# Four graph layers for 32 batches: how the last pair's attention weights are turned, weighed and divided

## The chip, the cores and the metric

The kernel runs on one core of one Trainium2 chip. Its engines work side by side, each through its own list of instructions in order: TensorE (PE, with its weight loads PEld), VectorE (DVE), ScalarE (ACT), GpSimd (POOL) and SyncE (SP), which here issues nearly all DMAs. The metric is the device time of one execution in microseconds (us); times on a profile page count from the start of the span.

## The reference

x has 32 batches of 512 nodes with 64 features; adj is a 512 x 512 graph with about 2% of its entries set. Four layers each add to x a function of h = relu(layernorm(x)). Layers 0 and 1 multiply by the graph and by small matrices. Layers 2 and 3 are attention:

```python
# layer 2: eight heads of the first gat_layer, then one more on their concatenation
h = x @ W
s = einsum('bnd,bmd->bnm', h, h) * graph
s = where(s == 0.0, -1e16, s)
a = softmax(s, axis=2)
out = einsum('bnm,bmd->bnd', a, h) + b          # leaky_relu 0.01 behind it
# layer 3
h = x @ weight
e = leaky_relu(h @ a[:D] + (h @ a[D:]).T, 0.2) * adj   # adj with ones on its diagonal
out = einsum('bij,bjd->bid', softmax(e), h) + bias
```

So each attention needs for every node a maximum over 512 scores, 512 exponentials and their sum, and then a sum of 512 rows of values weighed by the exponentials. TensorE can form that sum only with the weights turned, so that the summed node lies on the partitions.

## The kernel before, in words

Batches go in 16 pairs. A pair passes through `front` (layers 0 and 1 and the layer norms, in steps F0 to F32), the heads of layer 2 (units a, b, c, d, g, h, i, j; two units make a `Two`), the second attention of layer 2 (called f, or O), and layer 3 (called e, or L). Pairs overlap: while one is in its heads, the one before is in its O and L.

Every piece of work is a *job* with a name such as `15.x0O1` (pair 15, exponentials 0 of the O attention of batch 1). The order in which the jobs are written out is a list in the code: HEAD for the start, ROUND, which is repeated with a lag per job, and TAIL for the end, which begins in the middle of pair 12's heads. Nothing else orders the work: an engine takes its instructions as the list of jobs issues them, and waits at each for its inputs and for a free buffer. The letters: s scores, r maxima, m negated maxima, x exponentials, n normalise, t turn, v weigh, then u evict, t rows, r residual; oA, oB and oC are the layer norm behind O, oT, oE, oN and oV turn its result and form layer 3's values, de its target terms; aO and aL fetch rows of the graph; hQ, lQ and ZQ spread values over partitions by DMA. PSUM has four banks for scores and four for everything else; `mm_ps` gives a job the bank whose present user comes earliest in the list, by the table UNTIL.

An attention unit in general: scores come to PSUM; DVE (L678) multiplies them by the graph's factor and takes the maximum in one pass, at 128 rows x 512; POOL negates (L691); ACT takes exponentials with their sum (L698); DVE takes the reciprocal (L708) and POOL multiplies the 512 weights by it (L710); DVE turns blocks of 32 x 32 (L716); TensorE weighs with 32-row tiles (L725 for the heads, L953 for O and L of two neighbouring pairs). The 32-row tiles need the values with node 32 b + r on partition r, which the DMAs of `Spread` (L474) arrange.

The last pair has no neighbour behind it. Its O and L are cut into halves, one per batch (`Half`, L1026, with `HalfOut`, L1075, and `HalfLast`, L1133), of four tiles of 128 nodes, so that a batch can go on to layer 3 alone. A half of the last pair goes: scores (L1082 and L1087 for O; for L, targets at L1137 and then one ACT instruction per tile, L1143), maxima, negation for two tiles at a time, exponentials, normalisation on POOL, 32x32 turns on DVE, and then `weigh` (L1050): 64 matmuls with 32 x 64 values as weights and 128 columns of turned weights moving, into four PSUM banks. ACT (for L half of it DVE) evicts with the bias, L1067 and L1065; four TensorE turns (L1072) make rows of nodes again; DVE adds the residual (L1095, or L1150 with the output's DMA at L1151). The values for `weigh` are spread by `SpreadRows`: a store to DRAM (L1018) and four reads (L1023) per half, on SP's queue.

The other lines that are spoken of: L552 and L871 form layer 3's features and terms of pair 14, L863, L878 and L903 are SP's DMAs of its source and target terms (src, dst, pd), L907 its scores on ACT. L482 turns pair 14's result back, L934 and L935 add and store it. L1107 and L1117 are turns and layer 3's features of a half of pair 15; L504 is the aggregation over the graph in `front`; L820 turns a half's values.

Of the kernel before, what the change touches and what calls it, by code (L numbers as in the profile page):

```python
# [21 lines left out]
def gnn_stack_kernel(  # L22
# [36 lines left out]
        w03:y03 w13:y13 o3:c3 vAE:eu et:er oT:oE oN:oV oD:oF h0:H0 h1:H1 vAL:lu lt:lr vAO0:ouO0 otO0:orO0 oT0:oE0  # L59
        oN0:oV0 vAL0:ouL0 otL0:orL0 vAO1:ouO1 otO1:orO1 oT1:oE1 oN1:oV1 vAL1:ouL1 otL1:orL1  # L60
    """
    HEAD = """
        0.weights 0.F0 0.F1 0.F2 0.biases 0.F3 0.F4 0.joined 0.F5 0.F6 1.F0 0.graph3 0.graph0 0.graph1 1.F1 0.graph2
        0.F7 0.F8 0.bjoined 0.F9 0.F10 0.F11 0.F12 0.F13 0.F14 1.F2 0.F15 0.factor0 0.masks 0.F16 0.F17 0.grams
        0.F18 0.F19 0.F20 0.F21 0.F22 0.F23 2.F0 0.F24 0.F25 1.F3 0.factor1 0.factor3 0.F26 0.F27 1.F4 0.F28 1.F5
        1.F6 0.F29 1.F7 0.loops0 0.F30 0.F31 0.loops2 0.F32 0.zT 1.F8 0.zE 1.F9 0.vectors 0.k0 1.F10 0.Y0 0.factor2
        0.ZQ03 0.ZQ12 0.k1 0.s1a 0.s0a 0.r3a 0.r2a 0.r1a 0.r0a 0.ZQ02 0.m1a 0.s3a 0.r6a 0.r7a 0.x1a 0.s2a 0.m0a
        0.r4a 0.s1b 0.r5a 0.r2b 0.m3a 0.r3b 0.m2a 0.s0b 0.x0a 0.s2b 0.nAa 0.ZQ11 0.Y1 0.ZQ01 0.x2a 0.r0b 0.x3a 0.r1b
        0.r5b 0.m1b 0.k3 0.s1c 0.r4b 0.m0b 0.x1b 0.t0a 0.s3b 0.t1a 0.nBa 0.r3c 1.F11 0.r7b 0.x0b 0.r6b 0.m3b 0.t2a
        0.m2b 0.x3b 0.nAb 0.r2c 0.s3c 0.t3a 0.x2b 0.r6c 0.m1c 0.s2c 0.ZQ13 0.r7c 0.nBb 1.F12 0.Y3 0.x1c 1.F13 0.t0b  # L70
        0.t1b 1.F14 0.k2 0.ZQ00 0.Y2 0.t3b 0.s0c 0.t2b 0.r5c 0.r0c 0.vA0 0.r4c 0.r1c 0.s3d 0.m3c 0.m0c 0.m2c 0.s0d
        0.x3c 0.vB0 0.r0d 0.vC0 0.r1d 0.x0c 0.vD0 0.nAc 0.s1d 0.t0c 0.x2c 0.r6d 0.m0d 0.r7d 0.nBc 0.t1c 0.r3d 0.s2d
        0.us0 0.w10 0.r2d 0.r5d 0.r4d 0.w00 0.m3d 0.s1g 0.m1d 0.x0d 0.x1d 0.t3c 0.m2d 0.r2g 0.y10 0.nAd 0.s3g 0.x3d
        0.r3g 1.F15 0.x2d 0.r7g 0.t2c 0.r6g 0.nBd 0.y00 0.t1d 1.F16 0.m1g 0.t0d 0.o0 1.F17 0.t2d 0.s0g 0.m3g 0.c0
        0.x3g 0.t3d 1.F18 0.loops1 0.s0h 0.x1g 0.r1h 0.r0h 1.F19 0.vA1 0.vB1 1.F20 0.r0g 0.vC1 0.m0h 0.vD1 0.s2g
        0.r1g 0.s1h 0.us1 0.r5g 0.r4g 0.m0g 0.x0g 0.w01 1.F21 0.m2g 0.nAg 0.x2g 0.y01 0.w11 0.r2h 0.r3h 0.ZQ10 0.s3h
        0.m1h 2.F1 0.s2h 1.F22 0.x0h 0.x1h 0.nBg 0.t0g 0.y11 0.r7h 0.r6h 0.s0i 0.r5h 1.F23 1.F24 0.m3h 0.r4h 0.x3h
        0.m2h 0.nAh 0.t2g 1.F25 0.s1i 0.x2h 0.t1g 0.t3g 0.r1i 0.r2i 0.o1 0.t0h 0.nBh 0.t1h 1.F26 0.s2i 0.c1 0.r0i
        0.r3i 1.F27 0.t2h 0.t3h 1.F28 1.F29 0.s3i 2.F2 0.m1i 0.vA2 0.m0i 0.r5i 0.r4i 1.F30 0.m2i 0.x0i 0.r6i 0.vB2
        0.D0 0.x2i 1.F31 0.vC2 0.vD2 0.s1j 0.r7i 0.x1i 0.r3j 0.r2j 0.us2 1.F32 0.m3i 0.s0j 1.zT 3.F0 2.F3 1.zE  # L80
        1.ZQ01 0.m1j 0.s2j 0.r1j 0.r5j 0.w12 0.r0j 0.nAi 0.m0j 0.x3i 2.F4 0.r4j 0.nBi 0.s3j 2.F5 0.r7j 0.m2j 0.r6j
        0.t0i 0.y12 2.F6 1.k0 0.t1i 1.Y0 0.w02 0.m3j 1.s1a 1.s0a 1.r2a 1.r3a 0.x0j 0.x1j 2.F7 0.t2i 0.nAj 0.x2j
        1.r0a 0.t3i 0.t0j 1.m1a 0.x3j 0.y02 1.s2a 1.ZQ02 0.nBj 2.F8 1.r1a 1.k1 1.Y1 0.t1j 0.o2 1.s3a 0.t2j 0.t3j
        0.c2 1.ZQ00 1.r6a 0.vA3 1.r7a 1.r5a 1.s1b 1.m0a 1.r4a 1.m2a 1.s0b 1.m3a 0.vB3 1.x0a 1.r2b 1.x1a 0.vC3 1.nAa
        3.F1 1.x3a 1.x2a 1.nBa 1.r3b 1.r1b 1.r0b 1.t1a 1.m1b 0.vD3 1.s3b 1.m0b 1.ZQ03 1.t0a 1.r7b 0.f0 0.us3 1.s2b
        1.x1b 1.r6b 1.r4b 2.F9 1.x0b 0.loops3 1.r5b 1.s0c 0.w03 1.r0c 1.r1c 1.m2b 1.m0c 2.F10 1.s2c 1.nAb 1.r4c
        1.x2b 0.y03 1.r5c 1.m3b 1.t2a 1.s1c 0.w13 0.y13 1.r3c 1.x3b 1.t0b 1.r2c 2.F11 0.o3 1.nBb 2.F12 1.m2c 2.F13
        1.s0d 1.s3c 1.t1b 1.m1c 1.t3a 1.t2b 0.c3 0.f1 2.F14 1.t3b 1.r1d 1.r7c 0.hQ0 1.x0c 1.vA0 1.x2c 1.ZQ12 1.r0d
        1.r6c 1.s2d 1.m3c 1.m0d 1.x1c 1.nAc 0.D1 1.s1d 1.r3d 1.r2d 3.F2 1.r4d 1.m1d 1.x0d 1.t0c 1.r5d 1.vB0 1.x1d
        1.vC0 1.nAd 1.vD0 1.us0 1.m2d 1.t1c 1.s3d 1.x3c 1.r7d 1.r6d 0.s1f 1.nBc 1.t0d 1.m3d 0.r3f 1.w10 0.r2f 1.k2  # L90
        1.y10 1.Y2 0.hQ3 0.s0f 1.w00 2.F15 1.x2d 1.x3d 1.t1d 1.t2c 1.nBd 0.r1f 1.t3c 1.y00 0.s2f 1.t2d 0.m1f 2.F16
        1.t3d 2.F17 0.hQ2 0.r4f 2.F18 1.o0 0.s3f 0.x1f 1.c0 2.F19 0.r0f 0.r6f 4.F0 0.r5f 0.r7f 1.vA1 0.m0f 1.vB1
        0.x0f 0.m2f 2.F20 1.s0g 1.ZQ13 0.hQ1 1.s2g 1.vC1 1.vD1 0.m3f 1.r0g 1.r4g 2.F21 1.s3g 0.x2f 0.nAf 1.r5g 1.m2g
        1.us1 1.r1g 1.s1g 1.w01 0.x3f 1.w11 1.y01 1.r6g 1.m0g 1.r7g 1.s0h 0.t1f 1.r2g 0.nBf 0.t0f 1.y11 1.r3g 1.x0g
        0.t2f 1.x2g 1.m1g 1.r0h 2.F22 0.t3f 1.m3g 1.x1g 1.o1 1.s1h 1.r1h 1.nAg 2.F23 1.t0g 1.x3g 2.F24 1.nBg 1.ZQ10
        1.m0h 2.F25 1.s3h 1.c1 1.r7h 1.r3h 1.x0h 0.vAE 0.vBE 0.vCE 0.vDE 1.r2h 1.s2h 0.eu 1.t1g 1.t3g 1.r6h 1.m1h
        1.t2g 1.k3 1.r4h 1.m3h 0.et 1.Y3 1.r5h 1.x1h 1.s1i 1.m2h 0.er 1.s0i 1.x2h 1.ZQ11 1.x3h 1.r2i 1.nAh 1.r1i
        1.r0i 2.F26 1.s3i 1.t0h 1.nBh 2.F27 1.r3i 1.t1h 1.s2i 1.t2h 1.r6i 2.F28 1.r4i 1.m1i 1.m0i 1.x0i 1.x1i 1.s1j
        2.F29 1.t3h 2.F30 1.r5i 1.r7i 1.vA2 1.m3i 1.r3j 1.D0 1.m2i 1.x2i 1.vB2 2.F31 1.x3i 2.F32 1.vC2 1.nBi 1.r2j
        1.vD2 1.s2j 1.m1j 1.nAi 0.oA 1.r5j 1.us2 2.zT 2.zE 1.s0j 1.r4j 1.m2j 1.s3j 3.F3 1.w12 1.x1j 1.hQ0 3.F4 1.r1j  # L100
        1.hQ1 1.r0j 1.t3i 1.y12 1.m0j 4.F1 1.r6j 1.r7j 2.k0 1.w02 1.m3j 2.Y0 1.x0j 2.s0a 3.F5 1.t2i 3.F6 1.y02 0.oB
        2.s1a 2.r1a 2.k1 2.r0a 1.x2j 1.t0i 1.nAj 2.m0a 2.s2a 2.r3a 1.x3j 2.Y1 2.r2a 2.r5a 2.r4a 2.m2a 1.nBj 3.F7
        1.t1i 3.F8 1.t0j 1.t2j 1.o2 2.s3a 1.t1j 2.s1b 1.c2 1.f0 2.m1a 1.t3j 1.vA3 2.x1a 2.x0a 1.vB3 2.x2a 2.r2b
        2.nAa 2.r6a 1.vC3 1.vD3 2.r7a 2.m3a 2.x3a 2.s0b 2.t0a 2.r3b 2.t1a 1.us3 2.nBa 3.F9 2.r1b 2.ZQ03 3.F10 2.r0b
        2.ZQ02 1.w03 2.m0b 2.s3b 1.y03
    """
    ROUND = """
# [782 lines left out]
    class Last(Unit):  # L890
# [34 lines left out]
        def rows(self):  # L925
            self.pn = turned(self.yT)
# [449 lines left out]
```

## Time and profile before

| | us |
|---|---|
| median of 3 runs | 2054.76 (2052.51 to 2057.88) |
| the profiled execution | 2054.5 |
| its span, first to last instruction | 2052.6 |
| busy PE, DVE, ACT, POOL in the span | 1998.0, 1813.9, 1491.9, 1304.4 |
| mean granted TensorE clock | 0.992 |

The page has a line per engine with the span in 40 slices of 51 us, a digit for the tenths in which it was busy:

```profile
PE   6999999999999999999999999999999999999986
DVE  4788889999898999989899998999999899899965
ACT  1567678777787877778777787877778687777855
POOL 3466566757667576666757567675866766566543
PEclk9999999999999999999999999999999999999997
```

A row of the timeline or of the groups is to be read as: line, engine, operation, output<-inputs, tile (rows * columns of TensorE where there is one), partitions x elements, count. TensorE takes a float32 matmul in two records; a turn of 128 x 128 in one. A busy PE is not PE at its peak, since its matmuls overlap.

### The profile page before, as it was taken

The numbers are of one execution on the slowest core, as the hardware profiler recorded it, in microseconds if no ns is written. First come the engines' busy times: TensorE is split into PE (matmuls) and PEld (weight loads), VectorE is DVE, ScalarE is ACT, GpSimd is POOL, SyncE is SP. The second block draws the span as 40 slices with busy tenths as digits, with TensorE's granted clock in tenths as the row PEclk, the third lists the DMA queues.
The fourth block names the chain that finished last, engine by engine and source line by source line (L and its number), as shares of the span: only waits on it lengthen the run. The fifth ranks groups of instructions, "written<-read, shape, count | busy, mean of one in ns | idle before, by whom it ended". The sixth has DMA issues, their size and how long they took to land.

```text
span 2052.6 us, 91028 instructions
## 1 busy us (share of the span) xinstructions
PE 1998.0 (97%) x38941; PEld 1201.2 (59%) x38941; DVE 1813.9 (88%) x4170; ACT 1491.9 (73%) x3845; POOL 1304.4 (64%) x2211
## 2 busy tenths in 40 slices
PE   6999999999999999999999999999999999999986
PEld 4556565665656566565656656566565565665555
DVE  4788889999898999989899998999999899899965
ACT  1567678777787877778777787877778687777855
POOL 3466566757667576666757567675866766566543
PEclk9999999999999999999999999999999999999997
DMA  6101111111121110212111021211111121111222
GB/s 139 33 3 35 22 31 39 36 25 37 26 41 31 36 37 19 45 25 43 29 34 38 17 45 27 43 33 31 35 23 36 27 49 33 34 30 31 41 47 65
DMA packets 257625, 74.45 MB, mean 36 GB/s; under 512 B 240324, under 2 KB 249668, under 8 KB 257220
## 3 DMA queue, kind: packets, MB, share of 16 engines
q1 hardware_dynamic: 256768, 68.54, 16.1%
q8 instruction: 305, 5.00, 1.0%
q14 instruction: 100, 0.82, 0.1%
q10 hardware_dynamic: 452, 0.10, 0.0%
HBM read 16.52 MB, written 4.78 MB: 10 GB/s over the span
## 4 chain that ended last, share of the span: by engine, by line
PE 90%; DVE 4%; ACT 2%; issue 1%; DMA 1%; POOL 1%; SPq 0%; POOLq 0%; ACTq 0%; DVEq 0%
PE s L669 23%; PE mm L725 23%; PE mm L504 6%; PE s L672 6%; PE mm L527 5%; PE mm L786 5%; PE mm L953 5%; PE mm L766 5%; PE mm L1169 3%; PE mm L530 3%; DVE sm L678 2%; PE mm L552 2%; DVE sm L716 2%; PE mm L492 1%; PE mm L521 1%
## 5 line engine op out<-in xcount | busy, mean ns | idle before, releaser
L698 ACT ACTIVATE sm<-sm,nmx 128x512 f32<-128x512 f32 x1280 | 909.6, 716 | 183.0 <-POOL nmx L691 181.4
L710 POOL TENSOR_SCALAR sm<-sm,rs 128x512 f32<-128x512 f32 x1280 | 866.2, 696 | 231.0 <-DVE rs L708 212.4
L678 DVE CUSTOM_DVE_ANT_0 sm<-s,A 128x512 f32<-128x512 f32 x1264 | 803.7, 679 | 49.7 <-PE s L672 44.0
L716 DVE STREAM_TRANSPOSE sm<-sm 128x1024 f32<-128x1024 f32 x640 | 775.4, 1229 | 52.6 <-POOL sm L710 49.8
L669 PE MATMUL s<-ZZ,Y 64*64 64x512 f32 x4096 | 553.9, 597 | 1.6 <-DVE mx L678 0.9
L725 PE MATMUL mm<-sm,vq 32*64 32x256 f32 (+1 forms) x16640 | 485.8, 376 | 2.6 <-DVE rs L708 1.8
L725 PEld LDWEIGHTS mm<-sm,vq 32*64 32x64 f32 x16640 | 384.7, 132 | 117.7 <-issue 52.5
L691 POOL TENSOR_SCALAR nmx<-mx 128x2 f32<-128x2 f32 x640 | 131.1, 216 | 361.2 <-DVE mx L678 328.9
L698 ACT ACTIVATION_READ_ACCUMULATOR sm<-sm,nmx 128x1 f32 x1280 | 246.9, 193 | 0.0
L672 PE MATMUL s<-NEGM,I2b 64*64 64x512 bf16 x2288 | 242.2, 376 | 0.0
L669 PEld LDWEIGHTS s<-ZZ,Y 64*64 64x64 f32 x4096 | 144.2, 133 | 163.4 <-issue 72.2
L778 ACT ACTIVATE y<-mm,cols 128x512 f32<-128x512 f32 x256 | 161.2, 688 | 26.3 <-PE mm L766 26.1
L672 PEld LDWEIGHTS <-I2b 64*64 64x64 bf16 x2288 | 80.2, 107 | 152.2 <-issue 150.9
L447 POOL TENSOR_TENSOR r<-ve,mhalf 128x8 f32<-128x8 f32 (+1 forms) x65 | 106.3, 1636 | 49.8 <-DVE ve L445 49.7
L766 PE MATMUL mm<-us,Wh 64*64 64x512 f32 x1024 | 133.8, 590 | 1.5 <-ACT us L760 1.4
L760 ACT COPY us<-mm 128x256 f32<-128x256 f32 x256 | 75.9, 380 | 70.0 <-PE mm L725 69.9
L786 PE MATMUL mm<-y,Wo_sb 128*64 128x256 f32 x1024 | 124.1, 384 | 2.5 <-ACT Y L1180 2.5
L504 PE MATMUL mm<-AT,z 128*128 128x512 f32 x256 | 119.9, 612 | 4.5 <-DVE z L451 4.2
L527 PE MATMUL mm<-AT,v 128*64 128x256 f32 x1024 | 117.6, 382 | 0.1
L953 PE MATMUL mm<-sm,vq 32*64 32x256 f32 x3712 | 111.8, 376 | 2.0 <-DVE rs L708 0.7
L953 PEld LDWEIGHTS mm<-sm,vq 32*64 32x64 f32 x3712 | 101.5, 132 | 15.9 <-PE s L672 7.9
L678 DVE DVE_READ_ACCUMULATOR2_ANT mx<- 128x1 f32 x1280 | 106.0, 83 | 0.0
(166 smaller groups left out, 1849.0 us busy)
## 6 DMA issues: line engine op xcount, KB each, us to landing
vq<-z SPq DMA_DIRECT2D x512, 32.0 KB
HH<-cat SPq DMA_DIRECT2D x128, 64.0 KB
vq<-catT SPq DMA_DIRECT2D x240, 32.0 KB
vq<-h3n SPq DMA_DIRECT2D x240, 32.0 KB
A<-in_adj_dram SPq DMA_DIRECT2D x5, 1024.0 KB
xt<-in_x_dram SPq DMA_DIRECT2D x32, 128.0 KB
ZZ<-ZZ SPq DMA_DIRECT2D x32, 128.0 KB
out_dram<-xo SPq DMA_DIRECT2D x32, 128.0 KB
```

The costliest lines, as they stand in the source:

```text
L504: nc.tensor.matmul(pe, lhsT=v[:, m].rearrange("p j d -> p (j d)"), rhs=AT[:, m, :], start=(m == 0), stop=(m == NT - 1),)
L527: nc.tensor.matmul(ph[out_, :], lhsT=v[:, m, j, :], rhs=AT[:, m, h], start=False, stop=stop)
L669: nc.tensor.matmul(pss[half][R[ab], :], lhsT=lhsT, rhs=rhs, start=True, stop=False)
L672: nc.tensor.matmul(pss[half][R[ab], :], lhsT=I2b[R[half], :], rhs=NEGM[R[half], k, :], start=False, stop=True)
L678: nc.vector.tensor_tensor_reduce(self.sm[:, s, :], self.pss.pop(s), self.graph(s), 1.0, -FMAX, ALU.mult, ALU.max, self.small("mx", slice(s ...
L698: nc.scalar.activation(self.sm[:, s, :], self.sm[:, s, :], AF.Exp, bias=self.small("nmx", slice(s, s + 1)), accum_out=self.small("ssum", s ...
L710: nc.gpsimd.tensor_scalar(self.sm[:, s, :], self.sm[:, s, :], self.small("rs", slice(s, s + 1)), 1.0, ALU.mult, ALU.mult)
L716: nc.vector.transpose(out=two, in_=two)
L725: nc.tensor.matmul(self.u[i][R[c], 0 : weights.shape[1] * 32], lhsT=values[32 * i : 32 * i + 32, jb, :], rhs=weights[32 * i : 32 * i + 32, ...
L766: nc.tensor.matmul(self.py[ab][c][r, :], lhsT=Wh2[R[c], self.head(c, ab), r], rhs=self.us[R[c], 2 * ab : 2 * ab + 2].rearrange("p i (s e) ...
L786: nc.tensor.matmul(self.pa[R[half], 0 : N // 2], lhsT=Wo_sb[:, self.head(k, ab), :], rhs=self.y[self.head(k, ab)][:, half * N // 2 : (half ...
L953: nc.tensor.matmul(self.u[i][r, 0 : N // 2], lhsT=values[q, jb, :], rhs=unit.sm[q, :, 32 * jb : 32 * jb + 32], start=(jb == 0), stop=(jb = ...
```

## The change

- In the halves of the last pair the weights are no longer normalised and no longer turned by DVE. Each tile of 128 nodes goes alone: DVE negates its maximum (before POOL, two tiles at once), ACT takes the exponentials, TensorE turns the tile in four blocks of 128 x 128 into a PSUM bank, ACT and DVE copy half of it each back over the weights (`turned_kept`).
- `weigh` sums a tile's 512 nodes in four matmuls with 128 x 128 turned weights as the stationary operand and 64 columns of values moving. The result has the nodes on the partitions. So the evictions and the turns back are gone, and so is `SpreadRows` with its four stores and 16 reads: the values are used as they lie (`hn` and `h3n`).
- The division by the sum of exponentials comes last, on DVE: a reciprocal of 128x1 and one instruction that multiplies the weighed row by it and adds. For O it adds the bias, then ACT bends and DVE adds the residual. For L it adds x3, to which POOL has added the bias before (`biased`). The bias rows are fetched once by two DMAs. Layer 3's output goes in two DMAs per half, of two tiles each.
- PSUM: a half takes one bank per turned tile and one per two sums, where it took four for `weigh` and one for the turns back. UNTIL is changed to match.
- HEAD and TAIL are new orders. HEAD has the same 754 jobs. TAIL has the same jobs of pairs 10 to 14, and for pair 15 the new ones in place of the old; ROUND is the same. At the end of TAIL each engine's list is finer: behind the last head's first weighing TensorE has 56 jobs instead of 36, DVE 98 instead of 64, ACT 72 instead of 44, POOL 12 instead of 25, SP 11 instead of 31.

Some places in the two orders. Before, O0's weighing (`15.vAO0 15.vBO0`) stands ahead of pair 14's features (`14.oN`); after, the features and terms of pair 14 come first, and O0's four sums follow, then the scores of O1. Before, the layer norm of O1 (`15.oA1`) stands behind its residual; after, it stands behind pair 14's last turn (`14.t1e`). After, the first turn of L0 (`15.t0L0`) stands between pair 14's last weighing and `15.oT1`. In HEAD, `1.F3` (pair 1's transposes) moves ahead of `0.F21`, and `0.masks` from ahead of `0.F16` to behind `0.Y0`.

The diff, cut to its core:

```diff
-    class SpreadRows(Spread):
-        def store(self):
-            self.rows = dr.tile([N, D], F32, tag="rows", name="rows")
-            nc.sync.dma_start(out=self.rows.rearrange("(t q) d -> q t d", q=P), in_=self.source(0))
-        def quarter(self, i):
...
-            nc.sync.dma_start(
-                out=self.tile[32 * i : 32 * i + 32], in_=self.rows.rearrange("(b r) d -> r b d", r=32)
-            )
     class Half(Unit):
-        def weigh(self, part):
...
-                    nc.tensor.matmul(self.u[i][R[0], 0:P], lhsT=values[q, jb, :],
-                        rhs=self.sm[q, :, 32 * jb : 32 * jb + 32], start=(jb == 0), stop=(jb == JB - 1))
-        def evict(self):
...
-        def rows(self):
...
+        def negate(self, t):
+            one = slice(t, t + 1)
+            nc.vector.tensor_scalar(self.small("nmx", one), self.small("mx", one), -1.0, None, ALU.mult)
+        def exponentials(self, t):
+            nc.scalar.activation(self.sm[:, t, :], self.sm[:, t, :], AF.Exp,
+                bias=self.small("nmx", one), accum_out=self.small("ssum", one))
+        def turn(self, t):
+            pw = self.pws[t] = mm_ps()
+            for m in range(NT):
+                nc.tensor.transpose(pw[:, blk(m)], self.sm[:, t, blk(m)], ident)
+        def turned_kept(self, t):
+            pw = self.pws.pop(t)
+            nc.scalar.copy(self.sm[:, t, half[0]], pw[:, half[0]])
+            nc.vector.tensor_copy(self.sm[:, t, half[1]], pw[:, half[1]])
+        def weigh(self, t):
+            if t % 2 == 0:
+                self.pns[t // 2] = mm_ps()
+            values = state[self.p][self.values_of, self.j]
+            for m in range(NT):
+                nc.tensor.matmul(self.pns[t // 2][:, hblk(t)], lhsT=self.sm[:, t, blk(m)],
+                    rhs=values[:, m, :], start=(m == 0), stop=(m == NT - 1))
+        def divided(self, t, to, plus):
+            nc.vector.reciprocal(self.small("rs", one), self.small("ssum", one))
+            nc.vector.scalar_tensor_tensor(
+                to, self.pns[t // 2][:, hblk(t)], self.small("rs", one), plus, ALU.mult, ALU.add)
     class HalfOut(Half):
-        def residual(self):
...
+        def sums(self, t):                      # jobs z
...
+            self.divided(t, s["x3", self.j][:, t, :], s["bias"][:, 0, :])
+        def bent(self, t):                      # jobs p
+            nc.scalar.activation(y, y, AF.Prelu, alpha=0.01)
+        def residual(self, t):                  # jobs q
+            nc.vector.tensor_tensor(y, y, s["x2"][:, t, self.j, :], ALU.add)
     class HalfLast(Half):
+        def biased(self):                       # jobs b3
+            nc.gpsimd.tensor_tensor(x3, x3, s["bias"][:, 1:2, :].to_broadcast([P, NT, D]), ALU.add)
+        def residual(self, t):                  # jobs q
+            self.divided(t, self.xo[:, t, :], s["x3", self.j][:, t, :])
+            if t % 2:
+                two = slice(t - 1, t + 1)
+                nc.sync.dma_start(
+                    out=out[2 * self.p + self.j].rearrange("(t q) d -> q t d", q=P)[:, two], in_=self.xo[:, two])
+    def bias_rows(p):
+        state[p]["bias"] = bp.tile([P, 2, D], F32, tag="b", name="biasrows")
+        for k, b in enumerate((b_out, bias3)):
+            nc.sync.dma_start(out=state[p]["bias"][:, k, :], in_=b.partition_broadcast(P))
```

## The prediction

> **What bounds the kernel now.** I read the page's 40 slices first, then busy time by stretch, then the chain of waits over the end. TensorE (PE) is busy 97% of the span, and in the middle it never stands; its idle time lies at the two ends.
>
> The end by stretch (columns: time, length, busy us with counts of PE, PEld, DVE, ACT, POOL, then granted clock, DMA share, GB/s):
>
> ```profile
> 1850.00:1980.00 130.00, 125.70 (x2421) 71.82 (x2418) 119.56 (x272) 100.64 (x263) 80.76 (x150) 1.00 0.19 40
> 1980.00:2053.00 73.00, 47.29 (x964) 35.90 (x950) 38.32 (x94) 35.99 (x90) 20.71 (x36) 0.82 0.26 58
> ```
>
> In the first stretch PE stands 4.3 us of 130 and VectorE (DVE) is 92% busy. In the last 73 us no engine is over 65% busy: that part is a chain of latencies, and the granted clock falls to a mean of 0.82. The last 21 us of the chain, in order of time (start, us, what):
>
> ```profile
> 2030.97 1.03 PE s L1137 x4
> 2032.00 4.57 issue
> 2036.57 5.67 PE mm L1050 x109
> 2042.24 0.62 ACT yT L1067 x2
> 2042.86 0.10 issue
> 2042.97 0.45 PE mm L1072 x4
> 2043.41 0.66 issue
> 2044.07 0.21 PE mm L1050
> 2044.28 3.83 issue
> 2048.11 0.61 DVE yT L1065 x2
> 2048.72 0.14 issue
> 2048.86 0.45 PE mm L1072 x4
> 2049.30 0.02 issue
> 2049.32 0.42 DVE xo L1150
> ```
>
> One sees the last layer's two halves weighed one after the other (L1050, 5.7 us at the halved clock, then 4.1 us), each followed by an eviction and four turns back, then the sum L1150 and 2.9 us until the span ends. Ahead of it the half's tiles pass through normalise (POOL, L710, 0.69 us each) and 32x32 transposes (DVE, L716, 1.23 us per two tiles), and `weigh` can start only when all four tiles are through.
>
> **The change, part by part.** Per half of the last pair (four halves: O0, O1, L0, L1).
>
> Removed. POOL: 4 x 0.69 + 2 x 0.22 = 3.2 us. DVE: 2 x 1.23 transposes, 2 reciprocals of 0.15, one 128x256 addition of 0.41, and for L two evictions of 0.34: 3.2 us (O), 3.8 (L). PE: 128 records of L1050, 4.24 us at full clock, and four turns L1072 in 0.46: 4.7 us. ACT: 4 (O) or 2 (L) evictions of 0.36. SP: one store and four reads, 20 issues in all.
>
> Added. DVE: four negations and four reciprocals (as the 128x4 rows, 0.16 each), four copies of 128x256 (0.42), four divisions of 128x64; no row has this form, it lies between 0.16 (128x4) and 0.42 (128x256), and I take 0.22, a quarter of the way. That is 1.3 + 1.7 + 0.9 = 3.9 us, and for O four additions of the same size, 4.8. ACT: four copies of 128x256, 0.38 each, and for O four bends of some 0.3 (nearest row 128x128, 0.37). PE per half: four times four turns of 128x128, and four sums of four matmuls. The row L482 has the same four turns:
>
> ```profile
> 2017.92 1.97 PE L1117 MATMUL mm<-w3c,zT 64*128 64x66 f32 x8 [4.88 <-ACT zT L1111]
> ...
> 2029.19 0.75 PE L482 MATMUL mm<-ident,yT 128*128 128x128 f32 x4
> 2029.87 1.10 PE L1117 MATMUL mm<-w3c,zT 64*128 64x66 f32 x8
> ```
>
> 0.75 us includes a tail of 0.2, so 0.55 in a stream. A sum with 128 weights loaded for 64 moving columns does not occur; L1117 (128 columns of weights, 66 moving, eight records) is the nearest: 1.10 at full clock, 1.97 at half. I take 1.05. Four turns and sums: 6.4 us against 4.7, so PE does 1.7 us more per half. Lower bound: eight loads at the 0.14 us of the 128x128 rows of L820 as the only cost would be 1.1, and overlapped loads as with the 64x64 tiles of L552 (32 records in 0.9 us) only 0.25; upper bound eight loads at the 0.19 us of L504, 1.5, or 1.97 at half clock.
>
> The Trainium skill, "TensorE: Matmul & The Clock Gate", section "LDWEIGHTS (loading the stationary operand)", says that a weight load takes time by its columns, not its rows. Here a 32x64 load is 0.132 us (L725) and a 128x128 one 0.140 (L820): the doubled columns cost nearly nothing. By the page a 128-column load would be an estimated 0.107 us and the sum of eight 0.85.
>
> Now where these stand on the path.
>
> (a) From the last head's weighing (ends at 1980.6) to the end of its own projection nothing changes. Then the order of the jobs differs. Before, L1050 of O0 (1987.85, 4.24 us) stood on PE ahead of pair 14's L552 (1992.39); now pair 14's features go first. They are ready at about 1989, SP's four src issues (3.29 us) and dst follow, and pd can land at about 1997 instead of 2002.07. But on ACT the eight scores L907 now stand behind O1's exponentials, and those are late: O0's turns and sums (6.4 us on PE, plus 0.9 and 0.6 for L552 and L871) stand ahead of O1's scores L1082, which end at about 2000.5 instead of 1998.2. I walk O1: maxima to 2002.4, last exponential 2004.2. So the eight scores start at 2004.2 instead of 2002.07: the early pd is worth nothing, and 2 us are lost.
>
> (b) That loss is given back. Before, pair 14's exponentials waited on ACT for O1's late L1050 (it had waited 6.4 us for its vq, and ran at half clock) and its 1.12 us of evictions, and began at 2011.87 although the maxima were ready at 2009.4. Now ACT has eight scores of 0.63 to 2009.5, two copies, and begins at 2010.5; with 5.6 us of exponentials and a copy it ends at 2016.6 (before 2017.5). POOL's eight normalisations and DVE's four transposes follow as before: the last transpose ends at 2021.5 instead of 2022.4. Gain 0.9.
>
> (c) O1's layer norm now stands on DVE behind those transposes: 2021.5 plus 1.9 (four dependent steps as at 2012.98), maxima, POOL's 1.03, z at about 2026.6. PE's L725 (5.9 us) covers it until 2027.4. Behind that stand the first turn of L0 (0.55), and the features and nodes of O1. L1's first score comes at about 2032.3, before 2032.09. Sum of (a) to (c): 0, within 2 us either way.
>
> (d) The end. After L1's scores on PE (2032.2) there remain on PE 3 + 4 turns of 0.55 and 4 + 4 sums of 1.05: 3.9 + 8.4 = 12.3, with some 0.5 of waits for the last copies: 2045.0. ACT has 4 scores, 7 copies, 4 exponentials, 2.4 + 2.6 + 2.9 = 7.9; DVE four maxima 2.5, and four negations, seven copies and eight divisions, 0.7 + 2.9 + 3.0 = 9.1 from 2033. PE is the last. Then one division 0.4 and the output: 2.85 us by today's end, though it is half the bytes. End 2048.3, today 2052.6: **gain 4.3**.
>
> (e) The new order of the opening jobs and of pairs 12 to 15. PE is full from 100 to 1850 us, so order buys nothing there. In the first 100 us PE stands 21 us; I take 0 and bounds of 2.5 either way. In 1850 to 1980 it stands 4.3: losing as much again or gaining it all are the bounds.
>
> The normalisation on POOL and the 20 SP issues I cost at nothing: neither is late in today's end save O1's vq, counted in (b).
>
> **Sum.** The profiled execution took 2054.5 (span 2052.6 and 1.9 around it); minus 4.3 gives 2050.2. The median shown is 2054.76, 0.26 above; I forecast 2050.5.
>
> **Rivals.**
> 1. *More than that is won: 2046.7.* If the sums cost less than L1117 (loads hidden), DVE sets the end: from 2033 its 9.1 us and the waits for the last sum, about 2043, so 2.3 us less. And at 40.4 eight records of L504 take 5.26 us because the clock had halved; at its usual 0.468 each they take 3.74. The new order puts pair 1's transposes ahead of it; if they keep the clock, 1.5 us. For: PE's new pieces are short and nothing else is as late. Against: L1117 is the only such row and is bound by its loads. A replanned end that also saves some of the 4.3 us would go here.
> 2. *The clock stays halved through the end: slower than before, 2060.2.* Between 2028.3 and 2032.1 PE was 86% busy at clock 1.00, and stood from then; the clock was 0.5 by 2034 and full again only after 3.8 us of dense work from 2036.6, after 8.5 us from 2017.9. The new sums are loads with little streaming. If they don't lift the clock, the 12.3 us become 22.0 (by 1.97 to 1.10), 9.7 more. Each us at half clock loses 0.44, so it decides from 9.8 us on, where the gain of 4.3 is used up. For: L1117 and L1137 ran 4 us at half. Against: from 46 to 62 us PE was 42 to 100% busy in each 2 us and kept 1.00.
> 3. *No change within 1 us, 2054.* O1's late scores (a) are not given back, because the additional 4.8 us on DVE delays pair 14's maxima; then (d) pays.
>
> The skill's same page, section "Part 1: The HAM clock gate", has the clock halve after about 3.4 us idle and return after a like time of sustained work. The trace agrees in the return (3.8 and about 5 us, but 8.5 once), while the fall at 2033.6 came 1.6 us after the last matmul. By the page, PE working on from 2032 would keep full clock.
>
> **How the numbers follow.** Forecast 2050.5 with its own range 2047.5 to 2054: 0.45. Rival 1: 0.27. Rival 2: 0.13. Rival 3: 0.15. A difference of 0.3% (6.2 us) is about what this measurement can tell from no change. Faster by more than that needs under 2048.6: most of rival 1 and a part of the forecast's low side, 0.36. Slower needs over 2060.9: rival 2 with (e) against it, or O1's sums at half clock in (a) beside it, 0.11. Within: 0.53. Range: 2043 (rival 1 with both bounds of (e) partly in favour) to 2059 (half clock through most of the end).
>
> **What would show it.** Right: the stretch from the last L1137 to the end is about 16 us instead of 20.5, with no POOL normalising in it; eight records of a sum take 1.0 to 1.1; the clock is 1.00 after 2032; pair 14's L725 begins within 2 us of 2022. Wrong: sums of 2 us, a last transpose of pair 14 after 2024, or PE waits in 1850 to 1980 of over 9 us.

## The result, and the profile after

The changed kernel took 2047.24 us (median of 6 runs, 2046.47 to 2047.83) where the kernel before took 2054.40 in the same session (6 runs, 2052.51 to 2057.88): ratio 0.9964, 95% interval 0.9952 to 0.9976, a gain of 7.2 us. Forecast were 2050.5 and a gain of 4.3. The profiled execution has a span of 2044.9 us (before 2052.6), with a mean granted clock of 0.992 as before.

The page's slices of the changed kernel, 51 us each:

```profile
PE   6899999999999999999999999999999999999997
...
DVE  4778879999899999989999998999989989899967
ACT  1457658778787777878777787877878777787856
...
PEclk9999999999999999999999999999999999999998
```

PE's middle is unchanged; the first three digits are a little lower (less work done early), the last one higher. The end by stretch (time, length, busy us with counts of PE, PEld, DVE, ACT, POOL, then granted clock, DMA share, GB/s):

```profile
1850.00:1980.00 130.00, 126.41 (x2428) 74.19 (x2420) 120.53 (x276) 98.58 (x257) 82.25 (x149) 0.99 0.17 37
1980.00:2045.00 65.00, 50.08 (x679) 38.24 (x661) 38.99 (x139) 40.03 (x106) 11.16 (x18) 0.89 0.17 38
...
2031.00:2045.00 14.00, 10.54 (x92) 10.04 (x92) 8.27 (x35) 7.24 (x19) 0.00 (x0) 0.97 0.14 31
```

PE now stands 3.6 us between 1850 and 1980 (before 4.3). The last stage has lost 8 us of its length and about half of GpSimd's (POOL's) work, and in the last 14 us PE works for 10.5. The chain over that stage (start, us, what; here parts of it, pieces of 0.03 us and less left out unmarked) shows how they are used:

```profile
2031.00 0.67 ACT s L1155
2031.70 0.69 DVE sm L683
2032.39 0.60 DVE sm L683
...
2033.19 0.38 DVE sm L1054
...
2037.55 0.63 PE mm L1049 x4
2038.17 3.53 PE mm L1062 x32
2041.73 0.28 DVE xo L1073
2042.02 0.08 DVE rs L1072
2042.12 0.28 DVE xo L1073
```

Up to 2037.4 the chain runs through VectorE (DVE: maxima L683, copies L1054), with PE idle for 0.2 us in all between 2031 and 2041.7; then come the last turn L1049, four sums L1062 on end, two divisions L1073 and 2.5 us until the span ends. There is no eviction, turn back or GpSimd pass left in it. The pieces, from the timeline:

```profile
2036.35 1.04 PE L1049 MATMUL mm<-ident,sm 128*128 128x128 f32 x8
...
2038.01 3.68 PE L1062 MATMUL mm<-h3n,sm 128*128 128x64 f32 x32
```

Four records turn a tile in 0.52 us (the first and last ones with a tail, 0.66), eight records sum one in 0.92.

Where the time went, by three marks in the profiled runs, in us. "Heads end" is the end of the last head's weighing; "to L1" reaches from there to the first score of L1; "to the end" from there to the end of the span. In the timelines of before and after the marks are these (the first score of L1 after is in the chain above):

```profile
1972.74 7.74 PE L725 MATMUL mm<-sm,vq 32*64 32x256 f32 x256
...
2032.09 2.40 ACT L1143 ACTIVATE s<-s,src 128x512 f32<-128x512 f32 x4 [0.51 <-PE s L1137]
...
1974.19 7.74 PE L730 MATMUL mm<-sm,vq 32*64 32x256 f32 x256
```

The runs below the first two are the experiments:

| kernel | heads end | to L1 | to the end | span |
|---|---|---|---|---|
| before | 1980.5 | 51.6 | 20.5 | 2052.6 |
| after | 1981.9 | 49.1 | 13.9 | 2044.9 |
| new_oldhead | 1980.1 | 49.0 | 15.5 | 2044.6 |
| old_newhead | 1986.5 | 51.2 | 20.0 | 2057.7 |
| new_oldtail | 1981.4 | 49.3 | 13.9 | 2044.6 |
| old_newtail | 1978.4 | 52.5 | 20.6 | 2051.5 |
| new_last_only | 1980.0 | 53.2 | 15.4 | 2048.6 |
| new_out_only | 1979.0 | 48.5 | 20.1 | 2047.6 |
| pool_normalises | 1978.8 | 59.3 | 24.7 | 2062.8 |
| pool_two_factors | 1975.1 | 52.2 | 14.9 | 2042.2 |
| warm_one | 1978.8 | 48.9 | 14.1 | 2041.8 |
| warm_both | 1978.9 | 52.6 | 15.4 | 2046.9 |
| head_two_back | 1980.3 | 49.3 | 13.9 | 2043.5 |
| head_three_back | 1981.3 | 49.3 | 13.9 | 2044.4 |

A row is one execution and not the median: that of `pool_normalises` lies 7 us above its kernel's median, those of `new_oldhead`, `new_last_only` and `warm_both` about 2 above, and that of `pool_two_factors` is the fastest of its five.

So the end gained 9.1 us (2.5 and 6.6), and 1.4 were lost ahead of it. That loss hides two larger numbers. At one and the same instruction of the middle the changed kernel was 5.1 us late:

```profile
428.19 0.61 PE L521 MATMUL mm<-hT,W1T 64*64 64x256 f32 x8
...
433.27 0.61 PE L526 MATMUL mm<-hT,W1T 64*64 64x256 f32 x8
```

At a later one it was as late (L504 at 1447.36, L509 at 1452.44), and by the last head only 1.4: in these two executions the new start order lost 5, and the reordered pairs 12 to 15 gave 3.7 back.

### The profile page after: what moved, and what is told of

Same layout as the page of the kernel before. It is cut to its first block, busy times and chain, and to the rows that moved or that the text cites. A ratio compares the mean times of both kernels' runs of the same rounds, so it can differ in the third digit from the quotient of the medians.

```text
span 2044.9 us, 90347 instructions
## 1 busy us (share of the span) xinstructions
PE 1998.3 (98%) x38605; PEld 1202.3 (59%) x38605; DVE 1812.2 (89%) x4218; ACT 1493.2 (73%) x3857; POOL 1289.1 (63%) x2189
## 4 chain that ended last, share of the span: by engine, by line
PE 93%; DVE 4%; ACT 1%; POOL 1%; issue 1%; DMA 0%; SPq 0%; POOLq 0%; ACTq 0%; DVEq 0%
PE s L674 24%; PE mm L730 23%; PE s L677 6%; PE mm L509 6%; PE mm L791 6%; PE mm L958 5%; PE mm L532 5%; PE mm L771 5%; PE mm L1191 3%; PE mm L535 3%; PE mm L557 2%; DVE sm L683 1%; PE mm L497 1%; DVE sm L721 1%; PE mm L526 1%
## 5 line engine op out<-in xcount | busy, mean ns | idle before, releaser
L703 ACT ACTIVATE sm<-sm,nmx 128x512 f32<-128x512 f32 x1264 | 898.3, 717 | 163.6 <-POOL nmx L696 162.0
L715 POOL TENSOR_SCALAR sm<-sm,rs 128x512 f32<-128x512 f32 x1264 | 851.9, 693 | 208.9 <-DVE rs L713 171.2
L683 DVE CUSTOM_DVE_ANT_0 sm<-s,A 128x512 f32<-128x512 f32 x1264 | 803.9, 679 | 40.9 <-PE s L677 35.1
L721 DVE STREAM_TRANSPOSE sm<-sm 128x1024 f32<-128x1024 f32 x632 | 765.1, 1229 | 54.1 <-POOL sm L715 51.5
L509 PE MATMUL mm<-AT,z 128*128 128x512 f32 x256 | 121.4, 618 | 5.2 <-DVE z L456 4.5
L683 DVE DVE_READ_ACCUMULATOR2_ANT mx<- 128x1 f32 x1280 | 106.1, 83 | 0.0
```

The source lines that it names most:

```text
L509: nc.tensor.matmul(pe, lhsT=v[:, m].rearrange("p j d -> p (j d)"), rhs=AT[:, m, :], start=(m == 0), stop=(m == NT - 1),)
L683: nc.vector.tensor_tensor_reduce(self.sm[:, s, :], self.pss.pop(s), self.graph(s), 1.0, -FMAX, ALU.mult, ALU.max, self.small("mx", slice(s ...
L703: nc.scalar.activation(self.sm[:, s, :], self.sm[:, s, :], AF.Exp, bias=self.small("nmx", slice(s, s + 1)), accum_out=self.small("ssum", s ...
L715: nc.gpsimd.tensor_scalar(self.sm[:, s, :], self.sm[:, s, :], self.small("rs", slice(s, s + 1)), 1.0, ALU.mult, ALU.mult)
L721: nc.vector.transpose(out=two, in_=two)
```

## The experiments

Each kernel was timed beside the kernel before on the same chip; ratios are to that, with 95% intervals. In the first four the before took 2055.62.

### The two orders, alone and together

`new_oldhead` is the changed kernel with the start order (HEAD) of before; `old_newhead` is the kernel before with the changed HEAD. The edit of the first:

```diff
-        0.F0 0.F1 0.F2 0.weights 0.biases 0.F3 0.F4 0.joined 0.F5 0.F6 1.F0 0.graph3 0.graph0 0.graph1 0.graph2 0.F7
...
+        0.weights 0.F0 0.F1 0.F2 0.biases 0.F3 0.F4 0.joined 0.F5 0.F6 1.F0 0.graph3 0.graph0 0.graph1 1.F1 0.graph2
...
```

> The changed kernel with the opening order (HEAD) of the kernel before; TAIL and halves as changed. Theory A, from the two traces: the same repeated jobs of ROUND run 5.1 us later in the changed kernel (428.19 to 433.27 us at L521/L526, 1447.36 to 1452.44 at L504/L509), so the new HEAD costs 5.1 us, and this gives 2047.2 - 5.1 = 2042.1. Rival B, the prediction's (e): the opening order is worth nothing, 2047.2. Rival C: at 1980 us the lag is only 1.4 us, because waits later in the program take up a late start; then an early start is lost again and this gives 2045.8.

Measured: 2044.15 us (4 runs, 2042.21 to 2046.37), ratio 0.9946 (0.9931 to 0.9961), 3.1 us below the changed kernel's median, 3.7 by ratio; the two intervals overlap. The instruction at 433.27 came at 428.96.

> The kernel before with the changed kernel's opening order (HEAD), nothing else. Theory A: 2054.4 + 5.1 = 2059.5. Rival B: 2054.4. Rival C (the lag is mostly taken up by waits before the end): 2055.8.

Measured: 2059.25 (10 runs), ratio 1.0019 (1.0009 to 1.0028): slower than before by 3.6. The same instructions came at 433.90 and 1453.69.

`new_oldtail` has the new halves, HEAD of before, and TAIL in the old order as far as O0's first scores (`15.s0O0`); `old_newtail` is the kernel before with TAIL in the changed order as far as there. The edit of the second:

```diff
-        12.r5g 12.r6g 10.lQ2 11.nBf 12.m3g 11.t1f 12.r4g 12.x1g 12.s0h 11.t0f 12.c1 11.t3f 11.t2f 12.m2g 12.nAg
...
+        12.r4g 11.nBf 12.x1g 11.t0f 12.r6g 12.r5g 11.t2f 13.F23 12.s1h 12.s0h 11.t3f 12.r3h 12.m3g 12.m2g 13.F24
...
```

> The new halves of the last pair, with HEAD of before, and TAIL in the order of before as far as the first O scores of the last pair (job 15.s0O0); from there the changed order. Theory A: the halves and the order behind 15.s0O0 give 9.1 us (72.0 us from the last head's weighing to the end before, 62.9 after), so 2054.4 - 9.1 = 2045.3; the reordered pairs 12 to 15 give the other 3.7 (lag 5.1 in the middle, 1.4 at 1980). Rival B: orders are worth nothing, 2047.2. Rival C: the 3.7 us are the late start taken up, not the order; then 2054.4 - 9.1 = 2045.3 too, so it is the next run that tells A from C.

Measured: 2046.24 (4 runs), ratio 0.9957 (0.9942 to 0.9971).

> The kernel before with TAIL in the changed order as far as 15.s0O0 and its own order and halves from there; HEAD of before. Theory A: the order of pairs 12 to 15 is worth 3.7 us, 2050.7. Rivals B and C: it is worth nothing, 2054.4.

Measured: 2053.21 (10 runs), ratio 0.9987 (0.9977 to 0.9996), 2.4 us under before.

What follows: the order of pairs 12 to 15 is worth some 2 us (`old_newtail`; `new_oldtail` against `new_oldhead` gives as much, but their intervals overlap), and the start order costs 3 to 4 whichever halves go with it. The traces show it better. In ten runs with HEAD of before the instruction of the middle came between 426.1 and 429.5, in the two with the changed HEAD at 433.3 and 433.9. From the later instruction (1447.36 before) to the heads' end the eleven runs with the changed order of pairs 12 to 15 took 528.3 to 531.4 us and the three with the old one 532.8 to 533.7 (`before`, `old_newhead`, `new_oldtail`), whether they came early or late: 2.7 between the medians. So it is the order that gives time back, and a late start is not taken up by itself, as theory C had it. That the orders are worth nothing (theory B) is refuted; theory A holds, with sizes of some two thirds by the medians. The rest, 8 to 9 us, belongs to the halves and to the order behind `15.s0O0`, which cannot be had apart from them.

### Old O halves with new L halves, and the reverse

Both have HEAD of before and the changed order up to O0's scores. For `new_last_only`:

```diff
-                attn = HalfOut(p, j, "O", "rowsO", "hn")
+                attn = OldOut(p, j, "O", boc, AF.Prelu, "rowsO")
...
                 last = HalfLast(p, j, "L", "rowsL", "h3n")
```

`OldOut` is the kernel before's class, with its `SpreadRows`. Its jobs stand in the order of before up to L0's first score, and the new ones from there.

> The changed kernel with the start order of before and with the last pair's O halves as they were (normalised on GpSimd, turned on VectorE, spread by DMA); only the two L halves are of the new kind. Both kinds old under the same orders gave 2053.2 us, both new 2044.2. Theory A (the forecast's step d: the whole gain lies behind L1's first score): 2044 to 2045. Theory B (the trace: 6.6 us of the gain lie behind L1's first score, 2.5 before it, made by the O halves): 2046.7. Theory C (the halves gain only together, because the clock is kept only if neither leaves TensorE idle): over 2049.

Measured: 2048.84 (5 runs, 2044.58 to 2050.38), ratio 0.9965 (0.9951 to 0.9979); before took 2055.91 beside this kernel, the next two and `head_two_back`.

> The counterpart: O halves of the new kind, the two L halves as they were, start order of before. Theory A: 2053 (no gain without the L halves). Theory B: 2050.7. Theory C: 2053, with a low clock through the L halves.

Measured: 2049.99 (6 runs), ratio 0.9973 (0.9961 to 0.9984).

In the table each kind of half decides its own column: "to L1" is 51.2 to 53.2 with old O halves and 48.5 to 49.3 with new ones, whatever L is; "to the end" is 20.0 to 20.6 with old L halves and 13.9 to 15.5 with new ones, whatever O is (the two kernels with the division on GpSimd and `warm_both`, which change these stages themselves, are left out). The two gains add up to most of the whole (4.4 and 3.2 us under `old_newtail`, where both together have 9.1, each uncertain by some 3). A, by which the O halves gain nothing, falls with both runs. C falls with `new_out_only`, which it had at 2053; the median of `new_last_only` alone lies as near to C as to B. B fits both.

### The division moved back to GpSimd

`pool_normalises` undoes one part: the 512 weights of a row are divided by their sum before the turn, and the last instruction only adds.

```diff
             nc.scalar.activation(self.sm[:, t, :], self.sm[:, t, :], AF.Exp, bias=self.small("nmx", one), accum_out=self.small("ssum", one))
+            nc.vector.reciprocal(self.small("rs", one), self.small("ssum", one))
+            nc.gpsimd.tensor_scalar(self.sm[:, t, :], self.sm[:, t, :], self.small("rs", one), None, ALU.mult)
...
-            nc.vector.scalar_tensor_tensor(to, self.pns[t // 2][:, hblk(t)], self.small("rs", one), plus, ALU.mult, ALU.add)
+            nc.vector.tensor_tensor(to, self.pns[t // 2][:, hblk(t)], plus, ALU.add)
```

> The new halves with the start order of before (2044.2 us), but the exponentials are divided by their sum on GpSimd as the kernel before did (128x512 per tile) ahead of the turns, and the last instruction only adds. Theory A (the forecast: GpSimd's normalisation costs nothing, because something else is late): 2044.2. Theory B (it stands in the chain from exponentials to turns, about 0.9 us per half with its wait, in O1 and L1): 2046, with 0.9 us more from the last exponential to the last turn. Theory C (its 0.7 us per tile also slows VectorE beside it): 2047 or more.

Measured: 2058.29 (10 runs, 2054.22 to 2065.56), ratio 1.0017 (1.0004 to 1.0030). No theory had 14 us. The trace, of an execution that took 2065.19, shows two things. GpSimd's instruction took 1.56 us, where the same 128x512 in the heads takes 0.69 (L717; its code multiplies by the reciprocal and then by 1.0, the experiment's by the reciprocal alone). The rows give the shortest, the median and the longest in ns:

```profile
L1048 POOL TENSOR_SCALAR sm<-sm,rs x16: 1561/1562/1574, 1975.0 to 2050.4; 128x512 f32<-128x512 f32 x16
...
L717 POOL TENSOR_SCALAR sm<-sm,rs x1264: 681/692/731, 74.2 to 2023.9; 128x512 f32<-128x512 f32 x181
```

And the clock fell at 2038.6, in a pause of PE of 1.0 us, and did not come back (timeline of PE):

```profile
2036.97 1.08 PE L1149 MATMUL s<-zT,w3d 64*64 64x512 f32 x4
2039.08 1.12 PE L1053 MATMUL mm<-ident,sm 128*128 128x128 f32 x4 [1.03 <-POOL sm L1048]
...
...
2052.95 6.93 PE L1066 MATMUL mm<-h3n,sm 128*128 128x64 f32 x32
```

The last four sums took 6.93 us, where the changed kernel needs 3.68. `pool_two_factors` has the same edit with GpSimd's usual form:

```diff
-            nc.gpsimd.tensor_scalar(self.sm[:, t, :], self.sm[:, t, :], self.small("rs", one), None, ALU.mult)
+            nc.gpsimd.tensor_scalar(self.sm[:, t, :], self.sm[:, t, :], self.small("rs", one), 1.0, ALU.mult, ALU.mult)
```

> As the last kernel (new halves, start order of before, division on GpSimd ahead of the turns), but GpSimd's instruction is given a second factor of 1.0, as the kernel before had it: that form took 0.69 us for 128x512 at L717 of the same run, the one-factor form 1.56. The last kernel took 2058.3 us, with a clock of 0.5 from 2042 to the end; without GpSimd's division it is 2044.2. Theory A (the forecast: the normalisation itself costs nothing, what cost 14 us was the slow form, its lateness, and the clock it lost): 2044 to 2045. Theory B (in the chain, 0.9 us per half in O1 and L1): 2046. Theory C (any wait ahead of a half's turns drops the clock for the end): 2052 or more, eight records of a sum at 1.8.

Measured: 2047.63 (5 runs), ratio 0.9966 (0.9953 to 0.9979), before 2054.86 beside this kernel, the two with added turns and `head_three_back`. That is 10.5 us less than `pool_normalises` by ratio, and only the form of GpSimd's instruction differs. It is 4 us more than `new_oldhead` by ratio, though their intervals overlap. GpSimd's instruction took 0.69 again, and the clock was 1.00 through L1. The marks give 52.2 to L1 instead of 49.0, as long as with the old O halves, and 14.9 to the end. Its timeline in O1 (POOL's queue and PE's):

```profile
1998.19 1.52 POOL L1048 TENSOR_SCALAR sm<-sm,rs 128x512 f32<-128x512 f32 x2 [1.36 <-DVE rs L1047]
```

```profile
1996.89 0.66 PE L1053 MATMUL mm<-ident,sm 128*128 128x128 f32 x4 [1.23 <-POOL sm L1048]
1999.76 1.97 PE L1053 MATMUL mm<-ident,sm 128*128 128x128 f32 x8 [2.22 <-POOL sm L1048]
2001.52 3.52 PE L1066 MATMUL mm<-hn,sm 128*128 128x64 f32 x16
```

PE waits 2.2 us for GpSimd ahead of O1's last turns, and the clock falls there: eight turns in 1.97, sixteen sums in 3.52. But this wait and this fall are not what the division costs. Without it `new_oldhead` (first two rows) stood as long at the same place, for ScalarE, and lost the clock too; the changed kernel (last two) stood as long and kept it:

```profile
2001.63 1.52 PE L1051 MATMUL mm<-ident,sm 128*128 128x128 f32 x8 [2.18 <-ACT sm L1044]
2002.94 3.52 PE L1064 MATMUL mm<-hn,sm 128*128 128x64 f32 x16
...
2003.44 1.09 PE L1049 MATMUL mm<-ident,sm 128*128 128x128 f32 x8 [2.19 <-ACT sm L1042]
2004.37 1.90 PE L1062 MATMUL mm<-hn,sm 128*128 128x64 f32 x16
```

The cost shows when times are counted from the heads' end, against `new_oldhead`. O0's first turn begins 1.0 us later (PE waits 1.53 us for GpSimd instead of 0.54 for ScalarE); O1's last turns begin 3.1 later, since PE waits three times for GpSimd (0.56, 1.23 and 2.22) where it waited once; pair 14's weighing begins 3.1 later (41.0 instead of 37.9), and L1 3.2. So by this trace the division behind the sum is worth 1 us in O0 and 2 in O1. In L1 PE waits 1.2 us for GpSimd, and the stage is 0.8 to 1.0 longer than in the runs that kept their clock there (13.9 to 14.1); against `new_oldhead`, which lost it, nothing is left, so that part is not certain. Theory A, the forecast's "at nothing", fits neither trace nor median; B has the mechanism, but had a third of the cost ahead of L1.

### The clock

`warm_one` adds 14 turns of a constant, which nothing reads, ahead of O1's third turn; `warm_both` adds 24 more behind pair 15's first targets, and eight behind each of three of pair 14's 32x32 transposes. Both have HEAD of before.

```diff
+    def warm(n, source):
+        pw = mm_ps()
+        for i in range(n):
+            nc.tensor.transpose(pw[:, blk(i % NT)], source()[:, blk(i % NT)] if source else ident, ident)
...
-        15.t2O1
+        15.warm0 15.t2O1
```

> The changed kernel with the start order of before (2044.2 us), and 14 turns of a constant (0.13 us each) ahead of O1's third turn, where TensorE stood 2.2 us and the clock fell to 0.5 for the next 20 us. Theory A (TensorE's clock lies on the path here: O1's sums at 1.76 us per eight records instead of 0.92, features and targets twice as long): 2041 to 2042. Theory B (the stage is held by VectorE and ScalarE, whatever TensorE's clock): 2044.2, with clock 1.00 from 2002 to 2014. Theory C (the added turns delay O1's own): 2045 or more.

Measured: 2042.64 (4 runs), ratio 0.9946 (0.9931 to 0.9961), the same ratio as `new_oldhead`. The granted clock (last but two of the columns) held until O1's first two sums were done, as it did in the changed kernel without these turns:

```profile
2000.00:2004.00 4.00, 2.83 (x24) 2.69 (x24) 3.74 (x13) 4.00 (x9) 1.94 (x3) 1.00 0.26 56
2004.00:2008.00 4.00, 2.62 (x18) 2.38 (x18) 3.90 (x16) 4.00 (x12) 0.61 (x3) 0.87 0.44 94
2008.00:2012.00 4.00, 4.00 (x16) 2.65 (x15) 2.88 (x12) 4.00 (x15) 2.71 (x4) 0.50 0.29 66
```

The first two of O1's sums took 1.90 us instead of 3.52, and PE then waited 1.98 us more for VectorE's z. Pair 14's weighing began 37.9 us behind the heads' end, as in `new_oldhead`, where the clock was at 0.50 from 2002.1, and as in the changed kernel, where it was at 1.00 until 2009.9. In these rows ACT is busy for all of the 12 us and DVE for 10.5, PE for 9.5: ACT and DVE hold this stage, theory B. (B's full clock up to 2014 was not reached: it fell at 2007.0, behind the pause for z.)

> As the kernel with one group of added turns, and 24 more turns of the constant behind pair 15's first targets, and eight behind each of the first three of VectorE's transposes of pair 14, to hold the clock until pair 14's last weighing, which took 6.4 us at 0.5. Theory A (the weighing at full clock takes some 4 us): 2 us less than with one group, 2039 to 2040. Theory B: 2044.2, since what follows the weighing is late by another chain. Theory C (the clock has fallen already, the 48 turns take 0.26 us each and run into the weighing): 2046 or more.

Measured: 2046.40 (5 runs), ratio 0.9959 (0.9945 to 0.9973). Theory C, by this timeline:

```profile
2013.41 5.17 PE L1228 MATMUL mm<-ident 128*128 128x128 f32 x24
2018.42 2.78 PE L1228 MATMUL mm<-ident,sm 128*128 128x128 f32 x24
2021.14 2.86 PE L735 MATMUL mm<-sm,vq 32*64 32x128 f32 x179
```

The first 24 turns ran at half clock (0.22 us each), the clock came back at 2018, and the weighing at full clock was ready only at 2026.75, because it started 4.4 us later than in `warm_one`. Warming there costs what it brings.

### The start order

`head_two_back` moves two jobs of the changed HEAD to other places; `head_three_back` moves a third.

```diff
-0.zE 0.factor1 1.F9 0.vectors 1.F10 0.k0 2.F2 0.Y0 0.masks
+0.zE 1.F9 0.vectors 1.F10 0.k0 2.F2 0.Y0 0.factor1
...
-0.F15 0.factor3 0.F16
+0.F15 0.factor3 0.masks 0.F16
```

> The changed kernel, with two jobs of its start order moved: 0.factor1 from between 0.zE and 0.vectors to behind 0.Y0, and 0.masks from behind 0.Y0 to ahead of 0.F16, where before had it. The changed kernel takes 2047.2 us, with the whole start order of before 2044.2. Theory A (the loss of the new start order is these two VectorE jobs of 1.2 us each, ahead of the first scores): 2044.8. Theory B (the loss comes earlier, from pair 1's steps drawn ahead and the slower steps on GpSimd and VectorE up to z): 2047.2, and the first maxima still 4 us later than in the kernel before.

Measured: 2045.58 (4 runs, 2044.60 to 2047.50), ratio 0.9954 (0.9939 to 0.9969). How the first maxima are reached, on DVE in the changed kernel:

```profile
61.02 1.52 DVE L456 SCALAR_TENSOR_TENSOR z<-xc,r 128x512 f32<-128x512 f32 x1 [1.75 <-POOL r L452]
63.47 0.42 DVE L502 COPY ZZ<-mm 128x256 f32<-128x256 f32 x1 [0.93 <-PE mm L497]
63.81 1.22 DVE L390 SCALAR_TENSOR_TENSOR A<-A 128x1024 f32<-128x1024 f32 x1
...
72.20 0.69 DVE L683 CUSTOM_DVE_ANT_0 sm<-s,A 128x512 f32<-128x512 f32 x1 [2.98 <-PE s L677]
```

and in `head_two_back`:

```profile
60.52 1.52 DVE L458 SCALAR_TENSOR_TENSOR z<-xc,r 128x512 f32<-128x512 f32 x1 [1.75 <-POOL r L454]
63.32 0.42 DVE L504 COPY ZZ<-mm 128x256 f32<-128x256 f32 x1 [1.28 <-PE mm L499]
63.66 0.41 DVE L423 TENSOR_SCALAR w3T<-early,a 128x64 f32<-128x64 f32 x2
...
70.84 0.69 DVE L685 CUSTOM_DVE_ANT_0 sm<-s,A 128x512 f32<-128x512 f32 x1 [2.35 <-PE s L679]
```

In the changed kernel `0.factor1` (L390) stands ahead of the small copies that PE waits for; without it the first maxima come at 70.84, and the instruction of the middle at 431.93 instead of 433.27. Before they came at 68.19 and 428.19. So these two jobs are a part of the loss, 1.3 of some 5 us in that trace. The median is some 2 us under the changed kernel's, with overlapping intervals, so that the times alone do not show it.

> The changed kernel with three jobs of its start order moved: 0.factor1 and 0.masks as in the earlier run (2045.6 us, first maxima at 70.84), and 1.F8 from ahead of 0.F30 to behind 0.zT, where before had it, so that GpSimd's 128x512 step of pair 1 does not run beside VectorE's z (1.52 us beside it, 0.71 without). Theory A (the neighbour on GpSimd costs the 0.8 us): 2044.8, first maxima at 70.0. Theory B (the rest of the loss is in pair 1's and 2's other steps, and these come later whatever 1.F8 does): 2045.6.

Measured: 2046.87 (5 runs), ratio 0.9966 (0.9953 to 0.9979). It could not try its theory A: GpSimd's 128x512 step still ran beside z (61.15, z again 1.52 us), because that step is pair 2's `2.F2` and not `1.F8`. Moving `1.F8` brought nothing that these runs can show, and the two results overlap. What makes up the other 3 to 4 us is open. Two candidates in the traces, not tried, go with the order: z takes 1.52 us in all four runs with the changed HEAD or most of it and 0.71 in all ten with HEAD of before, GpSimd's r 2.55 and 1.65. Together they would be 1.7 us. A third is no cause by itself: the first aggregation (L509) took 6.70 us in the changed kernel and 5.25 before, but 5.22 in `head_two_back` and 6.17 in `new_oldhead`.

No kernel here is shown to be better than `new_oldhead` (ratio 0.9946), whose interval overlaps with that of the changed kernel (0.9964); `warm_one` equals it.

## Why the prediction was right and where it was wrong

The span forecast was 2048.3, the measured one 2044.9. By the forecast's own marks, with 1.4 us taken off where the heads end later: 2.7 us earlier at L1's first score (c), 2.1 less from there on (d), 1.4 later at the heads' end (e); 2.7 + 2.1 - 1.4 = 3.4. The direction and the main term held, the size was too small, and two steps were wrong in their reason: the normalisation on GpSimd, and the start order.

- **(a) to (c), "0, within 2 us either way": mis-sized, 2.7 us.** O1's last exponential was put at 2004.2 and ended at 2003.3, which is 2001.9 when the 1.4 are taken off. Everything behind moved with it: the eight scores began at 2003.29 (2001.9), pair 14's last transpose ended at 2019.72 (2018.3, forecast 2021.5), and its weighing began at 2019.82. One part is the sum: four took 3.68 in O0, not 4.2. The other lies ahead of it: pair 14's features ran at 1988.85 (1987.4), where the forecast had 1989. The forecast let this stage only balance; `new_out_only` shows that the O halves gain here whatever L does.
- **"The normalisation on POOL and the 20 SP issues I cost at nothing": failed for the normalisation.** Put back by itself (`pool_two_factors`) it cost some 4 us, 3 of them ahead of L1, where PE's turns wait for GpSimd in O0 and O1. With it L1 began 52.2 us behind the heads' end, as with the old O halves: in that trace it is the whole gain of the O halves. That PE also lost its clock in O1 is no part of it, by `warm_one` and the changed kernel. The SP issues were not tried alone.
- **(d), 16.0 us: the mechanism held, the size was 13.9.** PE is last, as forecast, with 10.54 us of work; by the profile's chain DVE leads up to 2037.4, so that both engines fill this stage. The sum was put at 1.05 us and is 0.92: 1.0 us over eight sums. The turns were nearly right (0.52 and 0.55). The waits of 0.5 and the output of 2.85 were each somewhat less (output 2.5). The division was put at 0.22 and is 0.28, the bend 0.26 (0.3). L1117, whose eight records took 1.10, was too dear a neighbour for the sum, whose eight records took 1.00 where they stand alone. The forecast's lower bound of eight loads one after the other, 1.1, was above its own 1.05 and above what was measured: it was no bound. The Trainium skill, "TensorE: Matmul & The Clock Gate", section "LDWEIGHTS (loading the stationary operand)", gave an estimated 0.85 for eight loads, an error of 0.07 against 0.13 by the row.
- **(e), "PE is full from 100 to 1850 us, so order buys nothing there; in the first 100 us 0, bounds 2.5": failed.** The start order cost 5.1 us by 428 us, twice the bound, and since PE is full behind it nothing wins it back before pair 12. A full engine is why a late start is kept, not why it is harmless. The order of pairs 12 to 15 gave 3.7 back (2.7 by all runs), within the 4.3 allowed. That these two nearly cancelled, and that the total came out near the forecast, is luck.
- **Rivals.** Rival 1's time (2046.7) came nearest, with one of its reasons: the sums are cheaper. Its other reasons did not hold: DVE led the end only up to 2037.4, and the clock at the first aggregation was not kept but lost for longer. Rival 2 did not happen: the clock was 1.00 from 2024 to 2044. That it can stay halved there is shown by `pool_normalises`, where the same stage took 24.7 us, GpSimd's slow form included. Rival 3 was wrong. The forecast read the clock's slowest return as 8.5 us of work; from 2017.9 to 2026.7 it was 8.8.

## What to carry to other kernels

Where every engine's order is written out and one engine is full in the middle, a microsecond lost at the start arrives at the end: compare one instruction in the middle of both traces before anything else, since the end can hide it. Where several stages follow, time each between its own marks in all runs; here that told the gain of each kind of half better than medians did. An operation on an idle engine is free only if nobody waits for its result: dividing 64 values behind a sum instead of 512 weights ahead of it took waits out of TensorE's path. And a fall of the clock is not a cost until a trace without it is shorter: here O1's sums took half the time at full clock, and the next stage began no earlier.

## What the runs showed that was not expected

- GpSimd multiplies 128x512 by a value per row in 0.69 us with a second factor of 1.0, and in 1.56 without it (L717 and L1048 of one run).
- In these traces TensorE's clock changed on a grid. The times at which it fell or rose, read from rows of 1 us (a mean of 0.91 from 2002 to 2003, with 1.00 ahead and 0.50 behind, means a fall at 2002.82): before 2002.82, 2009.66, 2016.48, 2026.72, 2033.54, 2040.38; after 2009.90, 2023.56; `new_oldhead` 2002.14, 2022.62, 2029.46, 2032.86. The distances are 1, 2, 3, 4 or 6 times 3.41 us, each within 0.02 us. The Trainium skill's page named above, section "Part 1: The HAM clock gate", says so: a free-running window of 3413 ns. So the length of a pause alone doesn't tell whether the clock falls: one of 2.2 us at the same place cost it in `new_oldhead` and not in the changed kernel. Two executions with the same L halves can differ so in L: `new_oldhead` lost the clock there for 3.4 us and took 15.5 us to the end, `warm_one` kept it and took 14.1.
- What fills a window enough is not settled. By the grid, a window in which PE was busy for 47% kept the clock (after, 1999.66 to 2003.07) and one of 82% lost it (`new_oldhead`, 2026.05 to 2029.46). The page has the clock at full after one busy window; in `pool_normalises` it stayed at 0.50 from 2038.6 to beyond 2060, with PE busy 20 of 21 us in its records, while in `new_oldhead` the same turns and sums brought it back within one window.
- VectorE's z with two operands took 1.52 us (61.02 in the changed kernel, shown above) beside a GpSimd step of 128x512 with two operands, and 0.71 before, where GpSimd ran another kind of step beside it, of 128x64 on one operand. The Trainium skill, "SBUF — State Buffer", section "Who interferes with whom", says that a VectorE instruction with two inputs from that memory contends with a GpSimd instruction reading it. The rows of the changed kernel agree; those of before show that not every step of GpSimd beside it costs z time. The rows of before (DVE, POOL), then POOL's of the changed kernel:

```profile
58.93 0.71 DVE L451 SCALAR_TENSOR_TENSOR z<-xc,r 128x512 f32<-128x512 f32 x1 [1.77 <-POOL r L447]
...
58.86 1.37 POOL L390 TENSOR_SCALAR_AFFINE_SELECT A<-A 128x64 f32<-128x64 f32 x4
...
60.95 1.04 POOL L460 TENSOR_TENSOR z<-xc,r 128x512 f32<-128x512 f32 x1
```
